# Projections issued in pairs, and their placing shared by ScalarE and VectorE

## The chip, the core and the metric

The kernel runs on one core of a Trainium2 chip. The metric is the device time of one execution in microseconds (us). A core has five engines with queues of their own: TensorE (PE; its weight loads are shown as PEld), VectorE (DVE), ScalarE (ACT), GpSimd (POOL) and SyncE (SP), which starts the DMAs here. TensorE writes its results into PSUM, eight banks of 512 float32 numbers in each of 128 partitions; VectorE and ScalarE read them from there.

## The reference

The input x is 16 images of 64 x 64 positions with 256 channels, in float32. Two layers follow each other:

```
x = x + linear_attention(group_norm(x))   # 8 heads of 32; softmax of q over a head's channels, of k over positions
x = x + local_attention(group_norm(x))    # 8 heads of 32; each position attends to its 7 x 7 neighbourhood
local_attention(x):
    q, k, v = x Wq + bq, x Wk + bk, x Wv + bv
    scores[n, j] = q[n] . (k[neighbour j of n] + e[j])      # 49 neighbours, e from emb0 and emb1, zero padding
    out[n] = sum_j softmax_j(scores[n]) v[neighbour j of n]
```

## The kernel before

The images are worked on one after the other. For each image `layer0` does the linear attention; then the values of the second layer are projected and stored to DRAM (`values`, L831 and L840), some projections of queries and keys are done (`AHEAD`), and `local_attention` does the rest. Its last steps overlap the start of the next image's `layer0`.

`local_attention` runs through eight passes k = 0 to 7 (`SEQUENCE`: four heads `hg` and a quarter `t` of the columns each). A pass has nine chunks of eight padded key rows, taken in five groups g of two (the last has one). A **step** is 5k + g, so there are 40 of them, and two more that finish. In one step the program issues, in this order:

- `place(step, FIRST)`: placing of earlier projections (below);
- `scores` of this group (L967, tiles of 64 x 64), into the two double banks `pd` in turn, each followed by the exponential on ScalarE (L976, L979);
- `place(step, LAST)`;
- the projection of this step's job, if its bank is `single[3]`;
- `weighted` for the group of the step before (L1011, tiles of 128 x 32; in the first step of a pass after a block L1022), with the copies of the result on ScalarE (L1110) in the first step of the next pass;
- the projection of this step's job, if its bank is `single[2]`;
- `summed` (L1050): sums of exponentials for the group before that, into `zs`, which is `single[2]` too;
- `both_chunks` on VectorE (L996): the exponentials of rows that two chunks share are added;
- `reciprocals` on VectorE (a transpose L1056, a reciprocal L1058), and at the end of a pass `finish` (a transpose L1063 on VectorE, then products and additions on POOL, L1071 to L1085);
- `between`: loads and stores on SP, and in some steps statistics of the next image's strips on VectorE (L522, in steps 10 to 17, 24, 27 to 30, 32 and 33).

A **job** is one projection of queries or keys that a later pass needs. `JOBS` gives one to each of 26 steps: none falls on a step with step % 5 == 4, and the last is job 31. `job_products` (L879) makes the matmuls, with tiles of 128 x 128: four for a job of keys, twelve for one of queries, as the profile counts them. `job_bank` gives jobs with step % 5 in (0, 2) the bank `single[2]`, and those with 1 or 3 the bank `single[3]`. `place_job` then moves the result head by head, adding a bias, into `kaug` (keys) or `qq` and `qx` (queries): on ScalarE (L755) or VectorE (L757). One head is one instruction, and two where the job is that of keys of strip 0 (jobs 6 and 21), since that strip is split into both edges of the image.

`placements` says when and where a job is placed. Each part is (how many steps later, FIRST or LAST, engine with 1 for ScalarE and 0 for VectorE, heads):

```
jobs 6, 21:         (1, FIRST, 0, (0, 1)), (1, LAST, 1, (2, 3))
n % 5 == 1, n < 31: (1, FIRST, 0, (0, 1, 2, 3))
n % 5 == 3:         (1, FIRST, 1, (0, 1)), (2, FIRST, 0, (2, 3))
others, and 31:     (1, FIRST, 1, (0, 1, 2, 3))
```

The order within the queues of TensorE, ScalarE, VectorE and SP is the order in which the program issues (`manual_schedule(engines=ORDERED)`); nothing overtakes. Waits between engines follow from what the instructions read and write.

Of the kernel before, what the change touches and what calls it, by code (L numbers as in the profile page):

```python
# [47 lines left out]
JOBS = {  # L48
    0: ("k", 0, 6),
    1: ("q", 0, 2, 0),  # L50
    2: ("q", 0, 2, 1),
    3: ("k", 0, 7),
    5: ("q", 0, 3, 0),
    6: ("k", 0, 0),
    7: ("q", 0, 3, 1),
    8: ("k", 0, 1),
# [22 lines left out]
FIRST, LAST = 0, 1  # L79


def placements():

    plan = {}
    for n, job in JOBS.items():
        if job[0] == "k" and job[2] == 0:
            parts = ((1, FIRST, 0, (0, 1)), (1, LAST, 1, (2, 3)))
        elif n % 5 == 1 and n < max(JOBS):
            parts = ((1, FIRST, 0, (0, 1, 2, 3)),)
        elif n % 5 == 3:  # L90
            parts = ((1, FIRST, 1, (0, 1)), (2, FIRST, 0, (2, 3)))
        else:
            parts = ((1, FIRST, 1, (0, 1, 2, 3)),)
        for later, when, engine, heads in parts:
            plan.setdefault((n + later, when), []).append((n, engine, heads))
    return plan
# [335 lines left out]
def attention_fast(tc, io, ok):  # L432
# [3 lines left out]
    with ExitStack() as ctx:  # L436
# [4 lines left out]
        single = [ps.tile([P, 512], F32, tag=f"ps{i}", name=f"ps{i}") for i in range(4)]  # L441
# [18 lines left out]
        n = Net(tc, cp, io)  # L460
# [42 lines left out]
        def strip(s):  # L503
            return slice(s * 512, (s + 1) * 512)

        def halves(b):

            return [img[0][0], img[1][b % 2]], [img[0][1], img[1][1 - b % 2]]
# [22 lines left out]
        def pieces(s):  # L531


            if s:
                yield s, 0, 8, 8 * s - PAD, lambda a: a.rearrange("p (r w) -> p r w", w=8)
                return
            for u, p0, m, n0, w in ((0, PAD, EDGE[0], 0, 0), (NB - 1, 0, EDGE[1], 16 * EDGE[0], W - EDGE[1])):

                def view(a, m=m, n0=n0):
                    part = a.rearrange("p (g n) -> p g n", g=4)[:, :, n0 : n0 + 16 * m]  # L540
                    return part.rearrange("p g (r w) -> p g r w", w=m)

                yield u, p0, m, w, view
# [310 lines left out]
        def job_products(job, x, to):  # L854
            what, hg = job[:2]
            if what == "k":
                parts = [(to, lambda a: a[:, strip(job[2])])]
            else:
                t, half = job[2:]
                image = to.rearrange("p (r w) -> p r w", w=16)  # L860
                parts = []
                for s in (2 * t, 2 * t + 1, 2 * t + 2):
                    for _, _, m, w, view in pieces(s % NS):
                        a, e = max(w, 16 * t), min(w + m, 16 * t + 16)
                        if a < e:
                            dst = image[:, :, a - 16 * t : e - 16 * t]
                            if s % NS == 0:
                                dst = dst.rearrange("p (g r) w -> p g r w", g=2)

                            def part(src, s=s % NS, view=view, a=a - w, e=e - w):  # L870
                                src = view(src[:, strip(s)])
                                if s == 0:
                                    return src[:, 2 * half : 2 * half + 2, :, a:e]
                                return src[:, 32 * half : 32 * half + 32, a:e]

                            parts.append((dst, part))
            for k in range(2):
                for i, (dst, part) in enumerate(parts):
                    nc.tensor.matmul(  # L879
                        dst,  # L880
                        (wq if what == "q" else wk)[:, k, hg * P : (hg + 1) * P],
                        part(x[k]),
                        start=(k == 0 and i == 0),
                        stop=(k == 1 and i == len(parts) - 1),
                    )
# [38 lines left out]
        def local_attention(b, x, y, after_scores, read, beside, between, stored):  # L924
# [67 lines left out]
            def both_chunks(hg, c, e, before):  # L992

                r0 = 8 * c - 2 * PAD
                part = rows_of(hg, c, e, r0, 8 * c)
                nc.vector.tensor_tensor(part, part, rows_of(hg, c - 1, before, r0, 8 * c), ALU.add)  # L996
# [16 lines left out]
            def place(step, when):  # L1013
                for n, engine, heads in PLACED.get((step, when), ()):
                    place_job(JOBS[n], single[job_bank(n)], engine, heads)

            def weighted(k, c, e):
                if c == 0:

                    for a, to in enumerate(outs):  # L1020
                        rows = slice(64 * a, 64 * a + 64)
                        nc.tensor.matmul(to, nb[rows], bits[rows, :1].to_broadcast([64, 512]), start=True, stop=False)  # L1022
                for j in range(2):
                    for h in range(4):
                        v = windows[k % 2][:, c, j, h * HD : (h + 1) * HD]
                        products(SEQUENCE[k][0], outs[j], j, h, c, e, *span(c), v, start=False, stop=(c == NB - 1))
# [64 lines left out]
            for step in range(len(groups) + 2):  # L1091
                new = None
                place(step, FIRST)
                if step < len(groups):
                    k, g = groups[step]
                    new = (k, g, [(c, scores(k, c)) for c in range(2 * g, min(2 * g + 2, NB))])
                    after_scores(step)
                place(step, LAST)
                if step in JOBS and job_bank(step) == 3:
                    job_products(JOBS[step], x, single[3])  # L1100
                if held:
                    k, g, es = held
                    for c, e in es:
                        weighted(k, c, e)
                    if g == 4:
                        rs[k] = [tail.tile([P, 1024], F32, tag=f"tail{i}", name=f"r{b}_{k}_{i}") for i in range(2)]
                        pvs = rs[k][1].rearrange("p (j n) -> p j n", j=2)
                        rs[k][1] = pvs
                        for j in range(2):
                            nc.scalar.copy(pvs[:, j], outs[j])  # L1110
                if step in JOBS and job_bank(step) == 2:
                    job_products(JOBS[step], x, single[2])
                beside(step)
                if late:
                    k, g, es = late
                    kept += es
                    for c, e in kept:
                        if c in LATE[g]:
                            summed(k, c, e)
                    kept = [(c, e) for c, e in kept if c not in LATE[g]]  # L1120
                if held:
                    k, g, es = held
                    for c, e in es:
                        if c:
                            both_chunks(SEQUENCE[k][0], c, e, before)
                        before = e
                if late:
                    k, g, es = late
                    if g == 0:
                        rc = small.tile([P, 32], F32, tag="rc", name=f"rc{b}_{k}")  # L1130
                    for a, at in enumerate((1, 2, 4)):
                        if g == at:
                            reciprocals(k, a, rc)
                    if g == 4:
                        finish(k, rc, *rs.pop(k))
                between(step)
                if held:
                    read(*held[:2])
                held, late = new, held

        def job_bank(step):
            return 2 + step % 5 % 2


        with tc.manual_schedule(engines=ORDERED):
            x, xn = halves(0)
# [39 lines left out]
            for b in range(B):  # L1186
                more = b + 1 < B
                x, xn = halves(b)
# [62 lines left out]
                def after_scores(step):  # L1251
                    if step == 19:
                        load_quarters(3, 4)
# [38 lines left out]
                def beside(step):  # L1292
                    nonlocal lower, steps
                    if more and step == 34:
                        steps = n.group_steps(st, 1e-5, small, lambda name: single[3], f"0_{b + 1}", gn)
                    if more and 34 <= step < 37:
                        next(steps, None)
                    if more and step == 39:
                        lower = layer0(b + 1, x_next, xn_next, *gn, 2)
                    if more and step >= 39:  # L1300
                        next(lower)
# [391 lines left out]
```

## Time and profile before

| | |
|---|---|
| median of 3 runs | 5272.87 us (5268.64 to 5277.87) |
| the profiled execution | 5278.82 us, its span 5276.9 us |
| TensorE clock granted | 0.993 |
| TensorE busy | 5114.0 us (97%) |
| VectorE busy | 2902.3 us (55%) |
| ScalarE busy | 2629.5 us (50%) |
| POOL busy | 1444.7 us (27%) |
| job matmuls L879 | 4096, of 245 to 636 ns (queries) and 592 to 1222 ns (keys) |
| placing, ScalarE L755 | 1888 instructions, median 679 ns |
| placing, VectorE L757 | 576 instructions, median 745 ns |

A line of a timeline gives the start and the duration in us, the engine, the line of the kernel, the operation, what it writes and reads, the shape, and how many instructions are merged; in brackets stands the idle time of the engine before it and who ended it. A matmul's duration contains its way through the array, so blocks overlap: the cost of a block is read from its start to the start of the next. A line of the waits gives who waited for whom, the total in us, how often, and the longest.

One image takes 5276.9 / 16 = 330 us. In the one from which the timelines are taken, the first scores start at 2170.08 us and the 40 steps end at about 2329.

### The profile page before, as it was taken

The page shows a single profiled execution, that of the slowest core. Times are in us where ns is not written, and L with a number is a line of the kernel's source. Part 1 is how long each engine was busy: PE and PEld are TensorE (multiplying, and loading weights), DVE is VectorE, ACT ScalarE, POOL GpSimd, SP SyncE. Part 2 cuts the span into 40 slices and gives each one's busy share as a digit, 9 for nine tenths or more (in the row PEclk, how much of TensorE's full clock was granted, in tenths as well). Part 3 has the DMA queues.
Part 4 walks back from the last instruction along what each step waited for, and adds up shares of the span by engine and source line. Part 5 has one row for each costly group of instructions (what it writes and reads, how often), then busy time and mean ns, then how long its engine had stood idle before and what let it go on. Part 6 is the DMA issues. An engine that isn't in the chain of part 4 may idle for free. (4 is left out here: it accounts for less than half of the span.)

```text
span 5276.9 us, 175070 instructions
## 1 busy us (share of the span) xinstructions
PE 5114.0 (97%) x76273; PEld 3770.1 (71%) x76273; DVE 2902.3 (55%) x5610; ACT 2629.5 (50%) x3569; POOL 1444.7 (27%) x2630
## 2 busy tenths in 40 slices
PE   7999999999999999999999999999999999999998
PEld 4776767777676776767767677676776767767676
DVE  5464555646546465464655646555465554745545
ACT  1552736527265372653726537174471744727346
POOL 3141231412314123140331403314032140422404
PEclk9999999999999999999999999999999999999999
DMA  5542625436154351543516445164441634417243
GB/s 134 124 119 51 146 64 128 116 56 150 52 131 115 71 135 49 131 117 72 131 49 135 115 80 134 42 138 107 93 122 43 148 95 103 123 43 150 82 92 88
DMA packets 763657, 537.33 MB, mean 102 GB/s; under 512 B 260656, under 2 KB 701616, under 8 KB 761200
## 3 DMA queue, kind: packets, MB, share of 16 engines
q1 hardware_dynamic: 721664, 515.94, 41.1%
q10 hardware_dynamic: 41216, 10.10, 1.2%
q8 instruction: 602, 9.86, 0.8%
q14 instruction: 175, 1.43, 0.1%
HBM read 367.11 MB, written 158.73 MB: 100 GB/s over the span
## 5 line engine op out<-in xcount | busy, mean ns | idle before, releaser
L996 DVE TENSOR_TENSOR e<-e,e 128x384 f32<-128x384 f32 x1024 | 684.3, 698 | 841.5 <-PE ps L1011 364.9
L755 ACT ACTIVATE qq<-ps,bias 32x512 f32<-32x512 f32 (+1 forms) x960 | 699.9, 734 | 812.5 <-DVE bias L750 657.5
L588 PE MATMUL pd<-wqkv,img 128*128 128x512 f32 x2048 | 926.6, 595 | 8.3 <-DVE img L359 8.3
L967 PE MATMUL pd<-qq,kaug 64*64 64x112 f32 (+5 forms) x24192 | 775.4, 267 | 44.0 <-issue 27.4
L967 PEld LDWEIGHTS pd<-qq,kaug 64*64 64x64 f32 x24192 | 673.3, 133 | 180.4 <-issue 92.7
L592 ACT ACTIVATE eq<-pd 128x1024 f32<-128x1024 f32 x256 | 261.9, 1023 | 1063.0 <-PE pd L588 1063.0
L501 POOL TENSOR_TENSOR others<-others,turn 128x9 f32<-128x9 f32 (+2 forms) x384 | 86.5, 225 | 2185.1 <-DVE turn L1056 2184.3
L588 PEld LDWEIGHTS pd<-wqkv,img 128*128 128x128 f32 x2048 | 387.4, 190 | 393.9 <-issue 350.5
L755 ACT ACTIVATE kaug<-ps,bias 32x512 f32<-32x512 f32 (+1 forms) x864 | 554.8, 651 | 181.2 <-PE ps L879 78.0
L979 ACT ACTIVATE e<-pd 128x896 f32<-128x896 f32 (+2 forms) x576 | 465.5, 835 | 227.8 <-PE pd L967 172.6
L595 DVE TENSOR_REDUCE qz<-eq 128x16 f32<-128x512 f32 x256 | 175.6, 686 | 706.5 <-ACT eq L592 706.5
L976 ACT ACTIVATE e<-pd 128x896 f32<-128x896 f32 (+2 forms) x576 | 463.5, 833 | 168.1 <-PE pd L967 114.8
L1011 PE MATMUL ps<-e,vbuf 128*32 128x112 f32 (+1 forms) x18432 | 529.7, 252 | 12.8 <-issue 12.8
L879 PE MATMUL ps<-img,wqn 128*128 128x160 f32 (+2 forms) x3072 | 536.3, 324 | 0.0
L879 PEld LDWEIGHTS ps<-img,wqn 128*128 128x128 f32 x3072 | 472.1, 190 | 55.9 <-DVE r L1063 10.5
L879 PE MATMUL ps<-img,w 128*128 128x512 f32 x1024 | 501.0, 614 | 0.8 <-DVE qq L757 0.3
L1085 POOL TENSOR_TENSOR img<-img,r 128x320 f32<-128x320 f32 (+1 forms) x512 | 489.1, 980 | 5.0
L606 PEld LDWEIGHTS ps<-vbuf,eq 128*128 128x128 f32 x2048 | 386.4, 190 | 144.7 <-issue 99.9
L1011 PEld LDWEIGHTS ps<-e,vbuf 128*32 128x32 f32 x18432 | 388.3, 110 | 140.7 <-issue 103.3
L606 PE MATMUL ps<-vbuf,eq 128*128 128x257 f32 x2048 | 485.1, 381 | 0.0
L831 PE MATMUL pd<-wvn,img 128*128 128x256 f32 x2048 | 468.1, 382 | 4.0 <-DVE hve L354 4.0
L831 PEld LDWEIGHTS pd<-wvn,img 128*128 128x128 f32 x2048 | 383.0, 190 | 67.7 <-issue 15.3
(142 smaller groups left out, 5577.7 us busy)
## 6 DMA issues: line engine op xcount, KB each, us to landing
vbuf<-vpad SPq DMA_DIRECT2D x1152, 96.0 KB
out<-img SPq DMA_DIRECT2D x256, 256.0 KB
vpad<-v SPq DMA_DIRECT2D x112, 512.0 KB
vbuf<-in_xt SPq DMA_DIRECT2D x158, 256.0 KB
img<-in_xc SPq DMA_DIRECT2D x75, 512.0 KB
img<-in_xc SPq DMA_DIRECT2D x106, 256.0 KB
qq<-pos SPq DMA_DIRECT2D x192, 128.0 KB
vbuf<-in_xt SPq DMA_DIRECT2D x60, 384.0 KB
```

What stands on the lines that cost most here:

```text
L588: nc.tensor.matmul(ps[:, t], xn[k][:, n0 : n0 + P], n.wqkv_sb[:, k, : 2 * C], start=(k == 0), stop=(k == 1))
L592: nc.scalar.activation(e, ps, AF.Exp)
L606: nc.tensor.matmul(pc[hg][:, : C + 1], eq[p][:, t, C + hg * P : C + (hg + 1) * P], tokens_of(p // 4)[:, 2 * (p % 4) + t], start=(p == 0 an ...
L755: nc.scalar.activation(dst, src, AF.Identity, bias=bias)
L831: nc.tensor.matmul(pi[:, t], x[k][:, n0 : n0 + P], wv[:, k], start=(k == 0 and t == 0), stop=(k == 1 and t == 1))
L879: nc.tensor.matmul(dst, (wq if what == "q" else wk)[:, k, hg * P : (hg + 1) * P], part(x[k]), start=(k == 0 and i == 0), stop=(k == 1 and ...
L967: nc.tensor.matmul(to, kaug[pl][rows, u, 8 * c : 8 * c + 8].rearrange("p r w -> p (r w)"), q, start=True, stop=True,)
L976: nc.scalar.activation(e.rearrange("p (a n) -> p a n", a=2), ps[:, :, : 2 * m], AF.Exp)
L979: nc.scalar.activation(e.rearrange("p (x r) -> p x r", r=hi - lo), src, AF.Exp)
L996: nc.vector.tensor_tensor(part, part, rows_of(hg, c - 1, before, r0, 8 * c), ALU.add)
L1011: nc.tensor.matmul(dst, stationary, pr, **flags)
L1085: nc.gpsimd.tensor_tensor(yv, xv, by_rows(add[:, :, a - w0 : e - w0], xv), ALU.add)
```

## The change

In steps with step % 5 in (0, 2) the job of the next step, whose bank is `single[3]`, has its projection issued immediately behind this step's own; in steps with 1 and 3 no projection is issued any more. Placing is shared in halves: a job of bank `single[2]` has heads 0 and 1 placed by ScalarE and heads 2 and 3 by VectorE at the start of the next step; a job with n % 5 == 1, job 31 among them, has heads 0 and 1 placed by ScalarE at the end of step n (LAST) and heads 2 and 3 by VectorE at the start of step n + 1. For jobs 6 and 21, and those with n % 5 == 3, the rule of placing stays.

```diff
@@ placements
         if job[0] == "k" and job[2] == 0:
             parts = ((1, FIRST, 0, (0, 1)), (1, LAST, 1, (2, 3)))
-        elif n % 5 == 1 and n < max(JOBS):
-            parts = ((1, FIRST, 0, (0, 1, 2, 3)),)
+        elif n % 5 == 1:
+            parts = ((0, LAST, 1, (0, 1)), (1, FIRST, 0, (2, 3)))
         elif n % 5 == 3:
             parts = ((1, FIRST, 1, (0, 1)), (2, FIRST, 0, (2, 3)))
         else:
-            parts = ((1, FIRST, 1, (0, 1, 2, 3)),)
+            parts = ((1, FIRST, 1, (0, 1)), (1, FIRST, 0, (2, 3)))
@@ local_attention
                 place(step, LAST)
-                if step in JOBS and job_bank(step) == 3:
-                    job_products(JOBS[step], x, single[3])
                 if held:
...
                 if step in JOBS and job_bank(step) == 2:
                     job_products(JOBS[step], x, single[2])
+                    if step + 1 in JOBS:
+                        job_products(JOBS[step + 1], x, single[3])
                 beside(step)
```

## The prediction

> **What bounds the kernel now.** I read first the busy times of the page, then TensorE's timeline over one image (start, duration, engine, line, operation), then the waits, then VectorE's and ScalarE's timelines at the steps that the change touches.
>
> ```profile
> PE 5114.0 (97%) x76273; PEld 3770.1 (71%) x76273; DVE 2902.3 (55%) x5610; ACT 2629.5 (50%) x3569; POOL 1444.7 (27%) x2630
> ```
>
> TensorE is busy 97% of the span, so the order and spacing of its work is the time. Below S is a block of scores (L967), W of weighted values (L1011), Z of sums (L1050), J a job's projection (L879). A step of the attention is S, J, W, Z or S, W, J, and the 16 images repeat to 0.1 us.
>
> ```profile
> 2152.48 1.88 PE L879 MATMUL ps<-img,w 128*128 128x512 f32 x4
> 2154.20 3.62 PE L831 MATMUL pd<-wvn,img 128*128 128x256 f32 x16
> 2157.65 1.99 PE L879 MATMUL ps<-img,wqn 128*128 128x160 f32 x12
> 2159.48 3.65 PE L831 MATMUL pd<-wvn,img 128*128 128x256 f32 x16
> ...
> 2195.15 1.98 PE L879 MATMUL ps<-img,w 128*128 128x512 f32 x4
> 2197.07 0.39 PE L1022 MATMUL ps<-bits,nb 64*128 64x512 bf16 x2
> 2198.74 1.56 PE L967 MATMUL pd<-qq,kaug 64*64 64x112 f32 x48
> ...
> 2201.14 2.09 PE L879 MATMUL ps<-img,wqn 128*128 128x160 f32 x12
> 2203.16 1.56 PE L967 MATMUL pd<-qq,kaug 64*64 64x112 f32 x48
> ```
>
> From start to the next block's start a J costs 1.72 us (keys) or 1.83 (queries) when work of the same shape, 128*128, follows, but 1.92 or 2.02 when a block with another tile shape follows. Each departure from 128*128 costs 0.19 us. The other seams: S 1.50, W before J 0.90, W before Z 0.79, Z 0.61 to 0.74.
>
> ```profile
> 2198.97 0.55 DVE L1056 STREAM_TRANSPOSE turn<-ps 128x352 f32<-128x352 f32 x1
> 2200.99 1.71 DVE L757 TENSOR_SCALAR kaug<-ps,bias 32x320 f32<-32x320 f32 x4
> ```
> ```profile
> 2202.73 1.74 ACT L755 ACTIVATE kaug<-ps,bias 32x320 f32<-32x320 f32 x4 [1.23 <-DVE kaug L757]
> ```
> ```profile
> ACT kaug L755 <- DVE kaug L757: 39.3, 32, 1.6
> ```
>
> This is step 7 of an image: job 6, the keys of strip 0, is placed. VectorE takes two heads once it is through step 6's reciprocals and transposes, and only then ScalarE the other two, though the heads lie in other partitions. That happens all 32 times that two engines share a job within one step: in this kernel, two engines' reads of one bank follow each other. The last read ends at 2204.47, which is 5.73 us after step 7's S began at 2198.74.
>
> ```profile
> 2302.45 1.57 PE L967 MATMUL pd<-qq,kaug 64*64 64x112 f32 x48
> 2305.75 1.70 PE L967 MATMUL pd<-qq,kaug 64*64 64x112 f32 x48 [0.84 <-ACT e L979]
> 2310.18 0.86 PE L1050 MATMUL ps<-e,ones 128*32 128x128 f32 x24
> ```
> ```profile
> 2304.70 1.27 DVE L996 TENSOR_TENSOR e<-e,e 128x384 f32<-128x384 f32 x2
> 2308.11 1.62 DVE L996 TENSOR_TENSOR e<-e,e 128x384 f32<-128x384 f32 x2 [0.95 <-PE ps L1011]
> 2309.66 0.47 DVE L1056 STREAM_TRANSPOSE turn<-ps 128x288 f32<-128x288 f32 x1
> ```
>
> Here are steps 32 to 34. TensorE waits for an exponential that stands behind job 31's four heads on ScalarE; and VectorE's transpose ends at 2310.13, just as step 34's Z, which overwrites that bank, begins.
>
> **What the Trainium skill says.** "TensorEngine Tiling (Array Packing)", section Key Properties: a change of tiling mode drains TensorE, a change of tile alone does not. The 0.19 us agrees. "PSUM — Partial Sum Buffer", section on bank collisions: engines must be kept apart by semaphores per bank and quadrant of partitions, per bank being the simple version. The 32 waits show the simple version. "TensorE: Matmul & The Clock Gate", section on what overlaps: matmuls start and end in program order. So what waits for a bank holds all behind it.
>
> **The change, part by part.** Thirteen pairs per image: jobs 1, 3, 6, 8, 11, 13, 16, 18, 21, 23, 26, 28, 31 move into the step before, behind the job there.
>
> *Fewer changes of shape.* S, J, W becomes S, W, and W, J, S becomes W, J, J, S. One departure less per pair: 13 × 0.19 = **−2.5 us** per image. The trace has no J directly before a J in these steps; the nearest row is a J before L831, of the same shape. The ends are 0 (the second J's first weights show) and 0.19 a pair; I take 0.19, since two J in a row before the attention show no gap either. No instruction is added on TensorE, and no DMA moves in SP's queue or operation in POOL's.
>
> *Placing.* Two heads take 1.38 us on ScalarE (half of 2.75) and 1.52 on VectorE. Per five steps ScalarE goes from ten heads to eight, VectorE from six to eight. ScalarE's share has cover: the first job of a pair is complete 2 us before the next step. So the small waits before steps 9 and 24, (3.6 + 4.5) / 16 = 0.5 us per image behind four heads on ScalarE, go, and a 0.1 in step 13: **−0.6**. In step 32 the seam W to S was 1.81 instead of 0.90 and the S after it 1.63 instead of 1.50: **−1.0**, as job 31 now leaves ScalarE before step 32's exponentials.
>
> *The strip-0 jobs, 6 and 21.* Their placing keeps its rule: step 7 (22), VectorE first, ScalarE last. Its start does not move against the end of step 6, since it stands on VectorE behind that step's transpose, reciprocal and L1063. But job 8 (23), which needs the same bank, moves from step 8 into step 7: it arrives S + W + J = 1.50 + 0.90 + 1.83 = 4.23 us after S began, and the bank is free at 5.73, plus 0.05 for the semaphore (an exponential's end to its S elsewhere). TensorE waits 1.55 us, twice: **+3.1**. Behind it stands the whole next step.
>
> *The other pairs.* The second job of a pair needs the bank from which VectorE placed two heads at that step's start. After a step of kind 1, VectorE is free 2.02 us after its transpose began (0.23 after S), or 2.58 with a strip's statistics between: ends at 0.23 + 2.02 + 1.52 = 3.77 or 4.33. Against 4.23 (4.12 where the job ahead is of keys), only steps 12 and 17, with statistics, are late, by 0.27 and 0.15. At steps 15, 25 and 30 the placing of the last job ended 3.4, 3.4 and 3.7 us after S, the second job arrives at 3.4: 0.1, 0.1, 0.3. Sums that wait for VectorE in 18 and 29: about 0.1 each. Together **+1.2**. This is an estimate from those rows; it could be 0 or 2.5, as POOL's overlap moves the 1.03 us of two L996 up to 2.5.
>
> *Step 32.* Two heads of job 31 now stand on VectorE ahead of L996. Its transpose ended 7.68 us after S(32); add 1.52, take off the 0.95 of idle: 8.25. Without ScalarE's wait TensorE arrives at Z(34) after 7.73 − 1.04 = 6.69. A new wait of **+1.6**, larger than the one removed.
>
> Sum per image: −2.5 − 0.6 − 1.0 + 3.1 + 1.2 + 1.6 = +1.8 us; 16 images: **+28 us**. The profiled execution took 5278.8 us (span 5276.9), so 5307; it stood 6 us above the median of 5272.9, to which the sum gives 5301. I take 5303.
>
> **The rivals.** *The bank wait is hidden* (faster). If VectorE were through with strip 0 early enough for ScalarE to end 4.2 us after S, the 16 × 3.1 = 50 us would vanish: 28 − 50 = −22, 5251 us. For it: VectorE has idle time in step 6, and the job's products are ready a step earlier. Against it: the in-order queue, where nothing ahead of the placing has moved. It decides once that chain ends 1.5 us earlier; at 0.5 us earlier two thirds of the wait are left. *All of it is hidden*: (2.5 + 0.6 + 1.0) × 16 = 66 us gained, 5207. Against it: VectorE is already at 15.8 of 20.1 us in steps 15 to 19, and the two heads more make 17.3. *VectorE becomes the bound* in every block with statistics or POOL beside it: another 0.5 us in five of the eight blocks, 40 us more, 5343. *The change doesn't save the shape changes*, because the second weight load of a pair shows: against it stand the rows above; 28 + 40 = 68, 5341.
>
> **How the numbers follow.** About 0.2% (10.5 us) is what a measurement tells from no change. The forecast has 0.70, bank wait hidden 0.12, all hidden 0.04, VectorE bound or no saving 0.14. Within the forecast the unknown waits (0 to 2.5 in the other pairs, ±0.5 at Z(34)) reach from 5275 to 5330, and some 0.08 of it lies within 0.2%. The range goes up to the last rivals, to 5345, and down to 5268, leaving the hidden cases out. Faster 0.15, same 0.09, slower 0.76.
>
> **What would show it.** Right: a J followed by J at 1.72 or 1.83; no [0.84 <-ACT e L979] at step 33; 32 waits of L879 for ScalarE's kaug L755, 1.5 us each, 50 us in sum; waits of L1050 for the turn L1056 of about 25 us; VectorE's L757 at 896 instructions (it has 576), ScalarE's L755 at 1568 (1888). Wrong: no row of L879 waiting for L755, or J to J at 1.9.

## The result, and the profile after

| | before | after |
|---|---|---|
| median of 6 runs | 5273.37 us (5268.13 to 5277.87) | 5355.4 us (5344.85 to 5360.09) |
| ratio | | 1.0144, 95% interval 1.013 to 1.0159 |
| span of the profiled execution | 5276.9 us | 5345.7 us |
| mean clock granted to TensorE | 0.993 | 0.990 |

The change makes the kernel 82 us slower by the medians and 69 us by the spans of the profiled executions. The forecast had the direction, and 28 us: about a third of it. S, W, Z and J below are the blocks of the prediction: scores, weighted values, sums, and the projection of a job. The page of the changed kernel shows that TensorE has the same instructions and that work went from ScalarE to VectorE:

```profile
PE 5105.4 (96%) x76273; PEld 3781.2 (71%) x76273; DVE 3179.1 (59%) x5930; ACT 2418.3 (45%) x3249; POOL 1437.7 (27%) x2630
```

The seams saved what was forecast. TensorE's timeline in step 20, a pair of queries and keys between other tile shapes:

```profile
2286.21 2.09 PE L879 MATMUL ps<-img,wqn 128*128 128x160 f32 x12
2288.14 1.91 PE L879 MATMUL ps<-img,w 128*128 128x512 f32 x4
2289.98 1.56 PE L967 MATMUL pd<-qx,kaug 64*64 64x112 f32 x48
```

From the first start to the scores the pair takes 3.77 us. Apart, the two took 2.02 + 1.92 = 3.94. The saving is spread over both, about 0.1 us each (1.93 and 1.84), where the forecast had all of it in the first (1.83 and 1.92). So a J of queries is followed by the next at 1.93, which the prediction named as a sign that it was wrong ("J to J at 1.9"); but it is the pair's sum that counts, and that is off by 0.02.

Step 22 places job 21, the keys of strip 0. VectorE's, ScalarE's and TensorE's timelines:

```profile
2293.35 0.55 DVE L1056 STREAM_TRANSPOSE turn<-ps 128x352 f32<-128x352 f32 x1
...
2295.36 1.71 DVE L757 TENSOR_SCALAR kaug<-ps,bias 32x320 f32<-32x320 f32 x4
```
```profile
2297.11 1.74 ACT L755 ACTIVATE kaug<-ps,bias 32x320 f32<-32x320 f32 x4 [1.21 <-DVE kaug L757]
```
```profile
2293.14 1.56 PE L967 MATMUL pd<-qx,kaug 64*64 64x112 f32 x48
...
2298.89 1.98 PE L879 MATMUL ps<-img,w 128*128 128x512 f32 x4 [1.26 <-ACT kaug L755]
```

ScalarE is done at 2298.85, 5.71 us after the scores began (forecast 5.73), and job 23's projection starts 0.04 us later. The step lasts 7.67 us; a step of the same work without the wait, step 2, lasts 6.17. So the wait costs 1.50 us, of which 1.26 stands in brackets (the idle time is counted from the modelled end of the matmul before).

Steps 32 to 35 are where the forecast falls furthest short. TensorE's timeline at steps 34 and 35 in the kernel before, the same in the changed kernel, VectorE's and POOL's timelines there, and the clock that TensorE was granted in three stretches (length, busy time with instructions, clock, DMA share, GB/s):

```profile
2310.18 0.86 PE L1050 MATMUL ps<-e,ones 128*32 128x128 f32 x24
2310.97 1.36 PE L967 MATMUL pd<-qq,kaug 64*64 64x64 f32 x48
2312.26 0.38 PE L1011 MATMUL ps<-e,vbuf 128*32 128x48 f32 x16
```
```profile
2341.60 0.97 PE L1011 MATMUL ps<-e,vbuf 128*32 128x112 f32 x32
2345.72 1.51 PE L1050 MATMUL ps<-e,ones 128*32 128x128 f32 x24 [3.15 <-DVE turn L1056]
2347.16 2.15 PE L967 MATMUL pd<-qq,kaug 64*64 64x64 f32 x48
```
```profile
2338.04 1.52 DVE L757 TENSOR_SCALAR kaug<-ps,bias 32x512 f32<-32x512 f32 x2
2339.59 2.23 DVE L996 TENSOR_TENSOR e<-e,e 128x384 f32<-128x384 f32 x2
2341.74 1.27 DVE L522 BATCH_NORM_STATS2 st<-img 128x6 f32<-128x512 f32 x2
2342.94 2.21 DVE L996 TENSOR_TENSOR e<-e,e 128x384 f32<-128x384 f32 x2
2345.18 0.48 DVE L1056 STREAM_TRANSPOSE turn<-ps 128x288 f32<-128x288 f32 x1
```
```profile
2338.15 1.88 POOL L1077 TENSOR_TENSOR r<-r,r 128x144 f32<-128x144 f32 x4 [1.09 <-DVE r L1063]
2339.99 2.42 POOL L1085 TENSOR_TENSOR img<-img,r 128x320 f32<-128x320 f32 x2
2342.37 1.01 POOL L1077 TENSOR_TENSOR r<-r,r 128x192 f32<-128x192 f32 x2
2343.45 2.24 POOL L1085 TENSOR_TENSOR img<-img,r 128x320 f32<-128x320 f32 x2
```
```profile
2341.60:2345.72 4.12, 0.97 (x36) 0.97 0.02 4
2345.72:2347.16 1.44, 1.44 (x25) 0.50 0.18 35
2347.16:2349.23 2.07, 2.07 (x52) 0.58 0.97 305
```

The sums wait 3.15 us for VectorE, twice the forecast 1.6, and then they and the next scores run at about half the clock: 1.44 us for sums that took 0.79 in the kernel before, 2.07 for scores that took 1.29. The sums show this in 10 of the 16 images (1.51 us in place of 0.86), and in two more the scores alone. In 15 images the wait is 2.5 to 3.2 us, and 12 of them have the half clock. The last image has no statistics to make for a next one: there the wait is 1.6 us, and the clock stays full. The Trainium skill, "TensorE: Matmul & The Clock Gate", Part 1, has TensorE's clock halved after an idle window of some 3.4 us; here gaps somewhat shorter than that were enough.

TensorE's waits, before (the last line is from the page: instructions, busy time and mean duration, then the idle time before them) and after, in total, times and longest:

```profile
PE ps L1050 <- DVE turn L1056: 0.9, 1, 0.9
PE pd L967 <- ACT e L979: 16.7, 32, 0.8
L967 PE MATMUL pd<-qq,kaug 64*64 64x112 f32 (+5 forms) x24192 | 775.4, 267 | 44.0 <-issue 27.4
```
```profile
PE ps L1050 <- DVE turn L1056: 47.8, 17, 3.2
PE ps L879 <- ACT kaug L755: 34.6, 29, 1.3
PE ps L879 <- DVE qq L757: 2.4, 14, 0.2
```

Where the time went, from the starts of the scores in TensorE's timeline (means over the images, times 16):

| part of an image | before, us | after, us | change x 16 | forecast x 16 |
|---|---|---|---|---|
| steps 0 to 23 (strip 0's wait is here) | 100.6 | 101.8 | +19 | +20 |
| steps 24 to 26 | 12.1 | 13.7 | +26 | -1 |
| steps 27 to 33 | 26.7 | 25.8 | -14 | -16 |
| steps 34, 35 | 4.1 | 8.4 | +68 | +26 |
| step 36 to the next image (15 times) | 182.8 | 180.7 | -32 | 0 |

The last row's change is the mean's times 15, as no image follows the last. Three rows were not forecast: over twice the loss in steps 34 and 35, a loss in steps 24 to 26, and a gain after step 36. In steps 24 to 26 all brackets but one name no engine, only "issue": TensorE stands still for nothing that the waits show. These issue stalls come to 31.4 us there, and to 11.1 in the kernel before.

### The profile page after: what moved, and what is told of

Its sections match the earlier page's. It is cut to its first block, busy times and chain, and to the rows that moved or that the text cites. A ratio compares the mean times of both kernels' runs of the same rounds, so it can differ in the third digit from the quotient of the medians.

```text
span 5345.7 us, 175022 instructions
## 1 busy us (share of the span) xinstructions
PE 5105.4 (96%) x76273; PEld 3781.2 (71%) x76273; DVE 3179.1 (59%) x5930; ACT 2418.3 (45%) x3249; POOL 1437.7 (27%) x2630
## 5 line engine op out<-in xcount | busy, mean ns | idle before, releaser
L755 ACT ACTIVATE qq<-ps,bias 32x512 f32<-32x512 f32 (+2 forms) x800 | 591.6, 746 | 792.5 <-DVE bias L750 649.4
L996 DVE TENSOR_TENSOR e<-e,e 128x384 f32<-128x384 f32 x1024 | 710.7, 724 | 273.3 <-PE ps L1011 261.1
L1011 PE MATMUL ps<-e,vbuf 128*32 128x112 f32 (+1 forms) x18432 | 532.5, 253 | 13.3 <-issue 12.4
L879 PE MATMUL ps<-img,w 128*128 128x512 f32 x1024 | 499.6, 613 | 41.8 <-ACT kaug L755 34.6
L755 ACT ACTIVATE kaug<-ps,bias 32x512 f32<-32x512 f32 (+1 forms) x704 | 446.5, 645 | 182.3 <-PE ps L879 82.5
L879 PEld LDWEIGHTS ps<-img,wqn 128*128 128x128 f32 x3072 | 473.7, 190 | 72.9 <-issue 19.8
L879 PE MATMUL ps<-img,wqn 128*128 128x160 f32 (+2 forms) x3072 | 523.6, 321 | 0.4 <-issue 0.4
L1085 POOL TENSOR_TENSOR img<-img,r 128x320 f32<-128x320 f32 (+1 forms) x512 | 499.5, 1001 | 5.0
L831 PEld LDWEIGHTS pd<-wvn,img 128*128 128x128 f32 x2048 | 382.9, 190 | 67.8 <-issue 15.3
```

The lines of the kernel that those rows point to most:

```text
L755: nc.scalar.activation(dst, src, AF.Identity, bias=bias)
L831: nc.tensor.matmul(pi[:, t], x[k][:, n0 : n0 + P], wv[:, k], start=(k == 0 and t == 0), stop=(k == 1 and t == 1))
L879: nc.tensor.matmul(dst, (wq if what == "q" else wk)[:, k, hg * P : (hg + 1) * P], part(x[k]), start=(k == 0 and i == 0), stop=(k == 1 and ...
L1011: nc.tensor.matmul(dst, stationary, pr, **flags)
L1085: nc.gpsimd.tensor_tensor(yv, xv, by_rows(add[:, :, a - w0 : e - w0], xv), ALU.add)
```

## The experiments

Each is compared with runs of the kernel before on the same chip (medians 5273 to 5278 us); the changed kernel stands at +82 us on that scale. The 95% interval of each difference is some 7 to 11 us to each side, so two experiments that lie less than about 13 us apart are not told apart. Steps and waits are read from one profiled execution of each kernel.

**Pairs with the old placing.** The four rules of `placements` are those of before. Against the changed kernel:

```diff
-        elif n % 5 == 1:
-            parts = ((0, LAST, 1, (0, 1)), (1, FIRST, 0, (2, 3)))
+        elif n % 5 == 1 and n < max(JOBS):
+            parts = ((1, FIRST, 0, (0, 1, 2, 3)),)
...
-            parts = ((1, FIRST, 1, (0, 1)), (1, FIRST, 0, (2, 3)))
+            parts = ((1, FIRST, 1, (0, 1, 2, 3)),)
```

> The pairs of the change with the placing of before. Theory (three waits of TensorE outweigh 40 us of saved shape changes): the wait of jobs 8 and 23 for strip 0's bank stays (1.5 us each, 50 us in all); the wait of step 34's sums for the transpose goes, since ScalarE places job 31; but VectorE places four heads of jobs 11, 16 and 26 (3.0 us from 0.23 + 2.02 us after S, 0.57 later with statistics), so jobs 13, 18 and 28 wait 1.7, 1.6 and 1.1 us, 70 us in all. Sum -40 + 50 + 70 = +80 us over before, 5353. Rival 'pairing gains nothing': 5393. Rival 'the halves in placing are the loss': no more than 5240.

Measured: 5375.97 us, ratio 1.0176 (1.0161 to 1.0191), +99 us. Its waits of TensorE:

```profile
PE ps L879 <- ACT kaug L755: 36.8, 32, 1.6
PE ps L879 <- DVE qq L757: 36.7, 32, 1.8
...
PE ps L879 <- DVE qx L757: 22.1, 16, 1.7
```

Steps 12 and 13 take 10.68 us where the changed kernel takes 9.40, steps 17 and 18 the same, 27 and 28 10.22 for 9.17. Against 9.07, the time of steps 2 and 3 with the seams saved, that is 1.6, 1.6 and 1.2: the forecast waits. And the wait of step 34's sums is gone (2.5 us for that step, 5.7 in the changed kernel). The expected sum was 20 us short; steps 24 to 26 take 13.3 us, 1.2 more than before, which is that much. So with pairs the halves in placing are worth 17 us on balance: they take away the waits for VectorE and bring the wait of step 34.

**Halves without pairs.** The placing in halves, the projections where they were. Since a job with n % 5 == 1 is then projected only in step n, its heads 0 and 1 are placed at the start of step n + 1, not at the end of step n as in the change. Against the kernel before:

```diff
-        elif n % 5 == 1 and n < max(JOBS):
-            parts = ((1, FIRST, 0, (0, 1, 2, 3)),)
+        elif n % 5 == 1:
+            parts = ((1, FIRST, 1, (0, 1)), (1, FIRST, 0, (2, 3)))
...
-            parts = ((1, FIRST, 1, (0, 1, 2, 3)),)
+            parts = ((1, FIRST, 1, (0, 1)), (1, FIRST, 0, (2, 3)))
```

> The placing in halves without the pairs: each projection stays where it was before the change, and jobs with n % 5 == 1, job 31 too, have heads 0 and 1 on ScalarE and heads 2 and 3 on VectorE at the start of step n + 1. Theory: no wait of projections for strip 0 (job 8 arrives a step later than in the changed kernel), the saved shape changes are gone; job 31's two heads stand on VectorE ahead of step 34's sums as in the changed kernel (3 us of wait, and the half clock after it), ScalarE's waits before steps 9, 24 and 33 go: +50 + 15 - 26 = +39 us, 5312. Rival 'the halves in placing are the loss': 5388 (the change's 75 us and 40 more). Rival 'pairing is the loss': 5273 or less.

Measured: 5334.05 us, ratio 1.0102 (1.0088 to 1.0117), +57 us. No wait for strip 0, and one long one:

```profile
PE ps L1050 <- DVE turn L1056: 48.6, 17, 3.2
```

The wait of step 34 is the placing's own doing, pairs or no pairs. Most of the 18 us over what was expected may lie in steps 24 to 26 (13.0 us, 15 us more over 16 images); that the halves bring more stalls there without any pair was not expected. The mean clock is 0.985.

**Strip 0 by the general rule.** In the changed kernel, jobs 6 and 21 are placed as the other jobs with n % 5 == 1:

```diff
-        if job[0] == "k" and job[2] == 0:
-            parts = ((1, FIRST, 0, (0, 1)), (1, LAST, 1, (2, 3)))
-        elif n % 5 == 1:
+        if n % 5 == 1:
             parts = ((0, LAST, 1, (0, 1)), (1, FIRST, 0, (2, 3)))
```

> The changed kernel, with jobs 6 and 21 placed by the rule of the other jobs with n % 5 == 1: ScalarE heads 0 and 1 at the end of step n, VectorE heads 2 and 3 at the start of step n + 1. Theory: VectorE's part ends 0.23 + 2.02 + 1.71 = 3.96 us after S, before job 8 arrives at 4.23; the waits of 1.3 to 1.5 us for ScalarE go, 16 x 2 x 1.5 = 48 us, to 5307. Rival 'the queue position of the pair is the loss, not this wait': the wait is taken over by VectorE's two heads, 5345 to 5355.

Measured: 5326.31 us, ratio 1.0103 (1.0086 to 1.0119), +49 us: 33 less than the change. Steps 7 and 8, and 22 and 23, take 9.07 us as a median for 10.57, the 1.5 of the forecast, and no wait of L879 for ScalarE is left. But the 48 us were not got: steps 24 to 26 took 14.6 us where the changed kernel took 13.7, 15 us over 16 images, and the part after step 36 took 0.9 more, 14 us. A wait was taken away, and issue stalls behind it grew.

**Job 31 on ScalarE.** In the changed kernel, heads 2 and 3 of job 31 go to ScalarE at the start of step 33:

```diff
+        if n == max(JOBS):
+            parts = ((0, LAST, 1, (0, 1)), (2, FIRST, 1, (2, 3)))
-        if job[0] == "k" and job[2] == 0:
+        elif job[0] == "k" and job[2] == 0:
```

> The changed kernel, with heads 2 and 3 of job 31 placed by ScalarE at the start of step 33 in place of VectorE at the start of step 32. Theory: VectorE reaches the transpose of step 34's sums before TensorE does; the wait of 3 us goes in every image (47 us), and with it the half clock that follows it in 11 of 16 images (about 15 us): 5355 - 62 = 5293. Rival 'only the wait goes, the clock falls elsewhere': 5308. Rival 'VectorE is the bound of these steps whatever it places': a wait of 1.5 us stays, 5325 to 5330.

Measured: 5319.36 us, ratio 1.0078 (1.0059 to 1.0097), +42 us: 40 less than the change, where 62 were expected. Steps 34 and 35 take 4.5 us for 8.4, or 62 us over the images: the wait and the half clock go in full, and the mean clock is 0.993 again. TensorE's timeline there (this kernel has two lines more, so L1052 is the line of the sums, L969 that of the scores):

```profile
2321.83 0.86 PE L1052 MATMUL ps<-e,ones 128*32 128x128 f32 x24 [0.20 <-DVE turn L1058]
2322.62 1.36 PE L969 MATMUL pd<-qq,kaug 64*64 64x64 f32 x48
```

But most of the gain after step 36 goes with them: that part takes 182.5 us (182.8 in the kernel before), and 12.9 us of issue stalls are back in steps 36 to 38, where the changed kernel has none.

**Both repairs.** The two edits above together.

> The changed kernel with both repairs: jobs 6 and 21 by the rule of the other jobs with n % 5 == 1, and heads 2 and 3 of job 31 on ScalarE at the start of step 33. Theory of three waits alone: the saved shape changes (40 us) and ScalarE's removed waits (25 us) stand against some 20 us of small waits for VectorE, 5230. Theory with a fourth term (TensorE's instructions arrive late in steps 24 to 27 and take back what the repairs give, 'issue' in the trace): the two repairs add as they were measured, -33 and -40 us from the changed kernel, 5285, with over 3 us per image of issue stalls and half clock in steps 24 to 27.

Measured: 5296.6 us, ratio 1.004 (1.002 to 1.006), +19 us, near the sum of the two, +9, and far from the -47 that the three waits alone would give. The runs spread from 5274 to 5327 us, and the profiled one is the fastest of them. Even in it, with both waits gone, steps 24 to 26 take 14.1 us, 2.1 more than before. TensorE's timeline in step 24:

```profile
2264.89 0.58 PE L1011 MATMUL ps<-e,vbuf 128*32 128x112 f32 x15
2266.62 0.67 PE L1011 MATMUL ps<-e,vbuf 128*32 128x112 f32 x17 [1.15 <-issue]
```

In the middle of one block of matmuls, with no engine named, TensorE stops. The DMA engines are full then: 1.32 of their capacity as the trace counts it in 2264.30 to 2268.00, and 0.98 in the 9 us before. In that time the refill that is issued after step 21 is under way: `load_quarters(0, 2)` loads rows of `qq` for two quarters of the positions, by eight DMAs in the trace (the expectation below says 16) from 2255.82 on. Of the 1066 packets in 2263.50 to 2266.62, 946 have under 512 bytes, as its rows of 64 float32 numbers do.

**Both repairs, the refill split.** Quarter 0 is refilled after step 21, quarter 1 after step 26, by six DMAs each. Against both repairs:

```diff
                     if step == 21:
-                        load_quarters(0, 2)
+                        load_quarters(0, 1)
+                    if step == 26:
+                        load_quarters(1, 2)
```

> As the one before, and the 16 DMAs that refill the rings of quarters 0 and 1 after step 21 are split: quarter 0 after step 21, quarter 1 after step 26. Theory that this burst delays the fetch of TensorE's instructions: the stalls of steps 24 to 27 fall by half or more, 25 to 40 us less than with both repairs, 5250. Rival 'the fetch is late whatever the DMAs do': no change, within 10 us. Rival 'the burst only moves': the stalls appear in steps 27 to 30.

Measured: 5236.78 us, ratio 0.9925 (0.9905 to 0.9945): 41 us faster than the kernel before, and 60 less than with the repairs alone. The same place:

```profile
2253.35 0.97 PE L1011 MATMUL ps<-e,vbuf 128*32 128x112 f32 x32
2254.14 0.84 PE L1050 MATMUL ps<-e,ones 128*32 128x128 f32 x24
2254.91 1.42 PE L967 MATMUL pd<-qq,kaug 64*64 64x64 f32 x48
```

Steps 24 to 26 take 10.9 us, and steps 27 and 28 9.23 as against 9.17: the stalls did not move there. The issue stalls of steps 24 to 26 fall from 35.1 us to 2.1. So it is the burst of DMAs that stops TensorE there. This is the version that beats both kernels.

**The kernel before, the refill split.**

> The kernel before with the same split of the refill. Its stalls in steps 24 to 27 are 1.1 us per image, so no more than 18 us can be had: 5262 if the burst is the cause, 5277 if not. It is the control for the split alone.

Measured: 5265.65 us, ratio 0.9971 (0.9959 to 0.9984), 12 us less. The control: the split alone is worth 12 us, so the repaired pairs are worth 29 more. The issue stalls of steps 24 to 26 fall from 11.1 us to 0.6.

**Statistics a step later.** In the changed kernel:

```diff
-MEASURED = {..., 30: (1,), 32: (2, 4), 33: (3,)}
+MEASURED = {..., 30: (1,), 33: (2, 4, 3)}
```

> The changed kernel with the statistics of two strips (1.27 us on VectorE) moved from step 32 to step 33, behind the transpose for which step 34's sums wait. Theory: that wait falls from 3.0 to 1.8 us, and a gap of 1.8 us no longer halves the clock: 16 x 1.2 = 19 us and some 15 us of clock, 5325. Rival 'the half clock comes from other gaps': 5340. Rival 'VectorE's later work then holds step 35': the gain is given back in steps 35 and 36, 5350.

Measured: 5333.12 us, ratio 1.0103 (1.0083 to 1.0124), +56 us: 26 less than the change, for 1.27 us of VectorE's work moved. Of the 2.2 us by which steps 34 and 35 get shorter, 1.5 are the wait, which is halved:

```profile
PE ps L1050 <- DVE turn L1056: 24.2, 18, 1.6
```

The mean clock rises from 0.990 to 0.992, and none of the 16 waits, of 0.9 to 1.7 us, is followed by the half clock. So a wait of 3 us costs more than its length; one of 1.5 lengthens step 34 by 1.6 against the kernel before, about its length. Step 35 still takes 2.3 us for 1.9 before; how much of that is VectorE's later work was not separated.

**The changed kernel, the refill split.**

> The changed kernel with the refill of quarters 0 and 1 split as in the two runs before, and nothing repaired. It measures how much of the change's loss is the burst's. Steps 24 to 27 take 13.7 us on the mean in the changed kernel and 12.1 in the kernel before; with the split 10.9 in both repairs. Theory: they fall to 10.9 here too, 16 x 2.8 = 45 us, while the wait for strip 0 (1.3 us in steps 7 and 22) and that of step 34 (3 us) stay: 5310. Rival 'the burst costs no more here than in the kernel before': 12 us, as there, 5345.

Measured: 5313.77 us, ratio 1.0075 (1.0058 to 1.0093), +38 us: 44 less than the change. Steps 24 to 26 take 10.9 us, as expected, their issue stalls fall from 31.4 us to 1.8, and the two waits stay:

```profile
PE ps L1050 <- DVE turn L1056: 45.5, 17, 3.2
PE ps L879 <- ACT kaug L755: 34.2, 29, 1.3
```

The same split gave 12 us in the kernel before. The difference, 32 us, is what the change pays to the burst beyond that, and it was missing from the forecast. It isn't the pairs alone: the issue stalls of steps 24 to 26 are 21.7 us with the pairs and the old placing, and 20.8 with the halves and no pairs.

## Why the prediction was right in direction and wrong in size

**What held.** *Fewer changes of shape*: 0.17 us a pair in the pair shown, for 0.19. *The strip-0 jobs*: 1.50 us for 1.55, by the chain that was named, ending within 0.02 us of where it was put. *ScalarE's cover*: the waits before steps 9 and 24 are gone, and that of step 33 too; L757 has the 896 instructions named and L755 the 1568. *The other pairs*: by the medians the second J starts 0.33 us late in step 12 and 0.22 in step 17, for 0.27 and 0.15. Steps 0 to 33 without 24 to 26 come to +5 us by the trace and +4 by the forecast. The wait for strip 0 shows as 29 waits and 34.6 us where 32 and 50 were named, as the brackets leave a part out. The rival of a hidden bank wait, and that of everything hidden, fall with it: when the wait was removed, the time fell.

**The term that was mis-sized: step 32.** Two steps of the prediction failed: this wait, put at +1.6 us and measured at 3.15 with half the clock behind it, and the issue stalls below, which were put at nothing. The forecast shifted VectorE's transpose by the 1.52 us of two heads, and by nothing else, to 8.25 us after the scores of step 32. It ended at 2345.66 - 2335.71 = 9.95, while TensorE would have been there at 2341.60 + 0.79 - 2335.71 = 6.68, as forecast (6.69). The two L996 pairs take 2.23 and 2.21 us, where they took 1.27 and 1.62. POOL was at work beside them before too; but later by two heads, the second operation of each pair lies wholly beside POOL's L1085 (from 2339.99 and from 2343.45 in the timeline above), and takes 1.45 and 1.44 us. Before, it took 0.82 us beside L1077, and 1.07 partly beside L1085:

```profile
2304.92 2.35 POOL L1077 TENSOR_TENSOR r<-r,r 128x144 f32<-128x144 f32 x4 [1.09 <-DVE r L1063]
2307.23 2.09 POOL L1085 TENSOR_TENSOR img<-img,r 128x320 f32<-128x320 f32 x2
```

The Trainium skill, "SBUF — State Buffer", section Who interferes with whom, says that an operation of VectorE with two inputs in SBUF contends with GpSimd's reads, and the trace agrees: L996 takes 0.56 us when POOL is idle. The forecast had named this overlap for the other pairs and left it out here. That makes 1.6 us into 3.15. And a rest of that length brought the half clock, which the forecast did not have at all. In steps 34 and 35 of the 16 images, the time multiplied by what the granted clock lacked comes to 23 us, and to nothing in the kernel before. With the 47 us of waits that is the row of the table, 68. (The mean clock fell by less, as the kernel before has more of the half clock after step 36.)

**The term that was missing: issue stalls.** The forecast counted TensorE's waits for engines only, and took the time in which TensorE waits for nothing named to stay as it was, without a reason; in steps 24 to 26 it went from 11.1 us to 31.4. The page before has 27.4 us of "issue" before the scores, and the prediction does not speak of it. What is shown is that these stalls hang on the burst: one and the same split is worth 44, 60 and 12 us in three kernels, and leaves 0.6 to 2.1 us of stalls in steps 24 to 26. The traces also show what the stalls end with. The page lists a DMA queue of kind "instruction" (packets, MB, share of the DMA engines' time):

```profile
q8 instruction: 603, 9.88, 0.8%
```

That is 65 bytes for each of TensorE's 152,546 matmuls and weight loads. Of the 441 issue stalls in the eleven profiles, 435 end 1.2 to 1.8 us after a packet of this queue has landed; at random moments within 15 us of them, one in nine does. With both repairs such a packet takes 1.33 us on the mean in steps 23 to 26, and 1.09 with the split as well. So TensorE waits there for its instructions, which come late beside the burst. Some stalls last 3.5 us, so that longer packets alone don't account for them; what else delays the packets was not measured. Nor is it shown why the change makes these stalls grow. It leaves steps 23 and 24 without a projection, so that many short matmuls follow each other there; but the halves alone, which leave the projections where they were, bring half of the growth.

**A gain that was not forecast.** From step 36 on the changed kernel takes 2.1 us per image less, 32 us in all. Half of it lies in steps 36 to 38, where the kernel before has 15.3 us of issue stalls and the changed kernel none. The other profiles agree: where step 34 keeps its wait of 3 us, these stalls come to 0.3 to 2.2 us, and where it does not, to 11.3 to 14.8 (4.0 with the halved wait). So a rest in step 34 takes the place of stalls that come a little later; why was not measured. The other half is luck of these two profiles: in the first layer of the next image the kernel before lost 17 us to the half clock, the changed kernel nothing, and the other nine anything from 7 to 21 whatever was changed. Together they hid a third of the loss.

Of the rivals, "VectorE becomes the bound" (5343) and "the change doesn't save the shape changes" (5341) were nearest in time, but neither is what happened: the first named five blocks with 0.5 us each, and what the forecast missed lies in steps 34 and 35 and in the stalls of steps 24 to 26; and the shape changes were saved.

## What to carry to other kernels

Moving a producer earlier is worth nothing until the release of its buffer moves too: list for each bank who reads it last, in which queue, and behind what. When an operation slides along its queue, read its duration again at the place where it lands, beside what will then run there. And where the bound engine shows stalls that name no engine, price them as a term of their own: work out what fills the DMA engines there, before changing what the bound engine does around it.

## What the runs showed of the hardware

A gap of 2.5 to 3.2 us in TensorE's work was followed by half the clock in 12 of 15 images of the changed kernel; in the one shown it cost 1.4 us beyond itself (1.44 us for 0.79, 2.07 for 1.29). Gaps of 0.9 to 1.7 us, 16 of them in step 34 with the statistics a step later, were not followed by it. VectorE's L996 took 0.56 us with POOL idle and 1.27 on the mean wholly beside POOL's L1085 (changed kernel). And TensorE's instructions came late beside a burst of DMAs: splitting the burst in two took 12 to 60 us off an execution, in three kernels.
